# Matmuls of zeros ahead of groups for which the planned order leaves TensorE idle

## The chip, the cores and the metric

The kernel runs on one core of a Trainium2 chip. A core has five engines that run their own instruction streams side by side: TensorE (PE, matmuls; its weight loads are listed apart as PEld), VectorE (DVE), ScalarE (ACT), GpSimd (POOL) and SyncE (SP, which issues DMAs here). They meet at semaphores. The metric is the device time of one execution in microseconds; lower is better.

## The reference

The program takes eight images of 256 channels by 32 x 32 pixels and passes each through four layers, every one of the form `x = x + layer(group_norm(x))`:

```python
x = x + _L0_conv_ref(_gn(x), ...)   # attention over pixels, 8 heads of 64, q and k normalised
x = x + _L1_conv_ref(_gn(x), ...)   # 3x3 convolution, 256 to 256 channels
x = x + _L2_conv_ref(_gn(x), ...)   # 3x3 convolution, 256 to 256 channels
x = x + _L3_conv_ref(_gn(x), ...)   # a mixer block, below
```

The mixer block normalises over channels, splits the channels into four branches of 64, and runs a selective scan in each: a projection to 128 channels, a short convolution, and then for 16 states per channel the recurrence

```python
h = dA_t * h + dBu_t        # along the 1,024 pixels
y_t = einsum('bds,bs->bd', h, C_t)
```

After the branches come a gate, a chain of short depthwise convolutions with projections, attention with 8 heads of 32, a projection, layer norm, gelu, a 3 x 3 depthwise convolution, another layer norm and a last projection. All data is float32.

## The kernel before

**Tiling.** An image is two tiles of 128 partitions (channels) by 1,024 (pixels). [...]The PSUM tiles are `big` (128 x 1,024, two of them, for nearly all projections, attention scores and layer norm sums), `acc` (128 x 512, one, attention values), `cv` (128 x 512, two, convolution products and small statistics) and `y` (128 x 512, one, the sum of the scan over states).

**Stages.** For each image the parts are recorded under a letter: A (`front_attention`), O (`front_out`), C (`front_convs`), N (`scan_layers` up to the scan), S (the scan), F0 to F3 and Z0 to Z3 (front and back of each branch), B (`back_layers`, with the second attention) and E (`back_out`, `back_end`). Parts of several images are worked on side by side.

**The scan.** `scan_steps` runs over 64 units per image (4 branches, 2 halves of 512 pixels, 4 groups of states, 2 channel groups). In each, VectorE forms `hs` from `du` and `bc`, ScalarE makes the two decays `da`, VectorE scans twice, and VectorE multiplies `hs` by `bc` again. `add_up` then adds up over states on TensorE: after each second unit, four matmuls with the constant `sel` as weights, each into 32 of the 128 rows of `y`, which use 32 of the array's columns each and stand side by side. After the fourth group VectorE reads `y` in `u<-u,half_d,y`, and the next half starts on the same PSUM tile. There are four `hs` tiles.

**The order.** No engine call is issued at once. `Recorded` and `Plan.record` write every call down as an operation; `arrange` puts them in one order; `Plan.issue` then issues them in that order and ties each engine's instructions to it, so every engine runs exactly the planned sequence. That is why nearly all instructions of the profile carry one line, L252, the call in `issue`. `arrange` works on groups: `gather` joins neighbouring matmuls of a stream into groups, `appraise` gives each a duration from formulas, and a loop takes, among the engines' best candidates, the one that can start first by these durations. In it `free[e]` is the time at which engine `e` is free, `start` the time at which the chosen group can begin, `spare[room]` the times at which the buffers of a pool tag become free, and `new_tiles(n)` the buffers that group `n` would be the first to use. It also carries a picture of TensorE's clock: in `pass_windows`, with windows of `WINDOW` (3,413.33 ns), the clock is taken to halve after a window with less than 0.42 of matmul time and to recover after one with at least 0.85.

```python
def pass_windows(time):
    nonlocal window, used, warm
    while (window + 1) * WINDOW <= time:
        share = used / WINDOW
        warm = share >= 0.42 if warm else share >= 0.85
```

Where the loop starts a matmul group later than `free[0]`, TensorE is idle by the plan; before the change nothing is done about it. What the chip does at run time follows the order, not the planned times: an instruction starts when its engine has done the one before and its semaphores allow it.

## Time and profile before

| | us |
|---|---|
| three runs | 5207.44, 5217.47, 5219.44 (median 5217.47) |
| the profiled execution | 5205.82 |
| its span, first to last instruction | 5204.1 |

| engine | busy, us | share | instructions |
|---|---|---|---|
| TensorE matmuls | 4700.7 | 90% | 18,998 |
| TensorE weight loads | 1917.1 | 37% | 18,998 |
| VectorE | 4115.6 | 79% | 5,650 |
| ScalarE | 2880.8 | 55% | 3,768 |
| GpSimd | 3.3 | 0% | 18 |

The mean granted TensorE clock is 0.941 of full speed. A float32 matmul of the program shows as two records in the profile, so 18,998 records are 9,499 matmuls; a row `x4` of `y<-hs,sel` is two matmuls. The costliest groups of matmuls:

| group | records | busy, us |
|---|---|---|
| acc<-p,v (attention values) | 3,072 | 827.8 |
| cv<-taps,w (convolutions) | 3,072 | 746.0 |
| big<-q,k (attention scores) | 2,048 | 586.3 |
| y<-hs,sel (the scan's sum over states) | 2,048 | 336.9 |
| big<-ident,ln_r (a row spread over partitions) | 384 | 55.7 |

How the views are read: the page cuts the span into 40 slices of 130 us and gives each engine's busy share in tenths, with the granted clock (PEclk) below. The chain of waits starts at the last instruction and goes back, at each step to what released it or to the instruction before it on its engine; its shares say which engine the end time hangs on. The order of time lists instructions of an engine with their start and duration, and in brackets the idle time before and what ended it. A view by stretches gives busy time and the granted clock between two times.

### The profile page before, as it was taken

What the parts mean: (1) busy time and instruction counts of PE and PEld (TensorE: products, weight loads), DVE (VectorE), ACT (ScalarE), POOL (GpSimd) and SP (SyncE); (2) the same over time, 40 slices, a digit from 0 to 9 for tenths busy, and PEclk for the clock granted to TensorE, in tenths of its full rate; (3) what the DMA queues carried; (4) which work ended last, traced back from release to release, by engine and by line L of the source; (5) the groups of instructions that cost most, each with busy time, mean ns of one, the idle gap of its engine ahead of it and who ended that gap; (6) DMA issues with size and microseconds to landing.
All of it is one profiled execution on the core that took longest, in us unless ns stands there. A gap on an engine that the chain in (4) does not pass through costs nothing.

```text
span 5204.1 us, 53545 instructions
## 1 busy us (share of the span) xinstructions
PE 4700.7 (90%) x18998; PEld 1917.1 (37%) x18998; DVE 4115.6 (79%) x5650; ACT 2880.8 (55%) x3768; POOL 3.3 (0%) x18
## 2 busy tenths in 40 slices
PE   8999879989999999999999999999999899698595
PEld 3363243243432534244442444325343343232222
DVE  3335989888888968979897788888877989999903
ACT  4426445646665565646666555655656556566342
POOL 0000000000000000000000000000000000000000
PEclk9999889999999999999999999899999999798696
DMA  4133344344343433433423343324433444344100
GB/s 134 46 100 110 121 151 127 95 125 134 106 125 101 144 100 108 126 102 126 131 91 107 106 142 125 112 74 141 123 109 108 125 131 157 98 126 126 66 18 23
DMA packets 256658, 575.15 MB, mean 111 GB/s; under 512 B 51192, under 2 KB 79224, under 8 KB 256384
## 3 DMA queue, kind: packets, MB, share of 16 engines
q1 hardware_dynamic: 167680, 431.11, 26.5%
q10 hardware_dynamic: 88704, 140.55, 8.8%
q8 instruction: 152, 2.49, 0.2%
q14 instruction: 122, 1.00, 0.1%
HBM read 483.18 MB, written 63.18 MB: 105 GB/s over the span
## 4 chain that ended last, share of the span: by engine, by line
PE 64%; DVE 23%; ACT 5%; issue 4%; DMA 3%; SPq 1%; DVEq 0%; ACTq 0%
PE big L252 36%; PE cv L252 14%; DVE hs L252 13%; PE acc L252 12%; PE y L252 2%; ACT p L252 2%; DVE room L252 2%; DMA rs<-inv 1%; DVE xt L252 1%; DVE u L252 1%; DVE st L252 1%; DVE xm L252 1%; SPq L252 1%; DVE p L252 1%; ACT taps L252 1%
## 5 line engine op out<-in xcount | busy, mean ns | idle before, releaser
L252 ACT ACTIVATE p<-big 128x1024 f32<-128x1024 f32 x1024 | 1013.4, 1019 | 556.1 <-PE big L252 487.7
L252 ACT ACTIVATE da<-dt,a_neg 128x512 f32<-128x512 f32 x1024 | 727.8, 720 | 721.6 <-DVE hs L252 584.8
L252 PE MATMUL acc<-p,v 128*64 128x512 f32 x3072 | 827.8, 622 | 31.3 <-ACT p L252 28.3
L252 PE MATMUL cv<-taps,w 128*128 128x256 f32 x3072 | 746.0, 393 | 40.3 <-DVE taps L252 29.4
L252 PEld LDWEIGHTS cv<-taps,w 128*128 128x128 f32 x3072 | 580.3, 194 | 295.6 <-issue 147.2
L252 DVE TENSOR_TENSOR hs<-du,bc 128x1024 f32<-128x1024 f32 x512 | 613.4, 1210 | 73.7 <-PE y L252 61.1
L252 DVE TENSOR_TENSOR_SCAN hs<-da,carry,hs 128x512 f32<-128x512 f32 x512 | 638.1, 1271 | 9.1 <-ACT da L252 8.2
L252 DVE TENSOR_TENSOR hs<-hs,bc 128x1024 f32<-128x1024 f32 x512 | 621.7, 1214 | 18.2 <-ACT carry L252 16.6
L252 PE MATMUL big<-q,k 64*128 64x512 f32 x2048 | 586.3, 654 | 31.3 <-ACT p L252 23.0
L252 DVE TENSOR_TENSOR_SCAN hs<-da,hs 128x512 f32<-128x512 f32 x512 | 608.9, 1210 | 5.0 <-ACT da L252 3.5
L252 DVE TENSOR_TENSOR p<-p 128x1024 f32<-128x1024 f32 x256 | 311.8, 1218 | 227.6 <-ACT p L252 164.7
L252 PE MATMUL y<-hs,sel 128*32 128x512 f32 x2048 | 336.9, 643 | 121.2 <-DVE hs L252 119.3
L252 PEld LDWEIGHTS acc<-p,v 128*64 128x64 f32 x3072 | 161.3, 136 | 590.7 <-issue 415.7
L252 PEld LDWEIGHTS big<-q,k 64*128 64x128 f32 x2048 | 160.3, 189 | 427.7 <-issue 207.7
L252 PE MATMUL big<-qk,qk 32*128 32x512 f32 x2048 | 298.1, 645 | 3.1 <-ACT qk L252 2.2
L252 PE MATMUL cv<-p,v 128*64 128x512 f32 x1024 | 276.9, 612 | 0.0
L252 PE MATMUL big<-xn,w 128*128 128x512 f32 x512 | 232.8, 600 | 2.8 <-ACT v L252 2.5
L252 PE MATMUL big<-o,w 128*128 128x512 f32 x384 | 182.5, 621 | 12.5 <-DVE o L252 12.2
L252 PEld LDWEIGHTS y<-hs,sel 128*32 128x32 f32 x2048 | 50.1, 111 | 337.8 <-DVE hs L252 187.6
L252 DVE SCALAR_TENSOR_TENSOR room<-room,vec,room 128x992 f32<-128x992 f32 (+1 forms) x128 | 156.7, 1224 | 10.0 <-ACT room L252 9.2
L252 PEld LDWEIGHTS big<-qk,qk 32*128 32x128 f32 x2048 | 82.3, 184 | 187.2 <-issue 140.1
L252 PEld LDWEIGHTS big<-xn,w 128*128 128x128 f32 x512 | 94.0, 190 | 130.0 <-issue 115.2
(234 smaller groups left out, 5038.5 us busy)
## 6 DMA issues: line engine op xcount, KB each, us to landing
bc<-bc SPq DMA_DIRECT2D x256, 512.0 KB
w<-wc ACTq DMA_DIRECT2D x384, 256.0 KB
dt<-dt_m SPq DMA_DIRECT2D x128, 512.0 KB
du<-du_m SPq DMA_DIRECT2D x128, 512.0 KB
rs<-inv SPq DMA_DIRECT2D x64, 256.0 KB
raw<-xm SPq DMA_DIRECT2D x64, 256.0 KB
dt_m<-dt SPq DMA_DIRECT2D x128, 128.0 KB
du_m<-a SPq DMA_DIRECT2D x128, 128.0 KB
```

The lines of the kernel that those rows point to most:

```text
L252: made = op["call"](*args, **kwargs).ins
```

## The change

`arrange` now notes, when it takes a matmul group (`e == 0`) that starts over 1,000 ns after TensorE is free by the plan, whose first output has at least 128 elements a partition and lies in a pool tile whose buffer is free by then, a count: `0.75 * idle - 500` ns, divided by 220 ns. `issue` issues that many calls of `fill` ahead of the group's first matmul, each tied into TensorE's order like any other. `fill` calls the same matmul with a 128 x 128 tile of zeros as weights (as many rows and columns as the real matmul uses) and 128 columns of the identity as moving data, into the first 128 columns of the place that the group's first matmul will write. Where that matmul starts a sum, so does the fill, and is overwritten; where it continues one, the fill adds zeros. The order of all other operations, and the count of everything else, is as before.

```diff
+            for call in [self.fill] * idle + [op["call"]]:
+                made = (call(op) if call == self.fill else call(*args, **kwargs)).ins
...
+    def fill(self, op):
+
+        out, lhs = op["outs"][0], op["ins"][0]
+        rows = slice(region(lhs)[1], region(lhs)[2])
+        zeros, moving = self.still
+        moving = moving[rows]
+        if len(out.shape) == 3:
+            wide = out.shape[2]
+            out = out[:, 0 : P // wide]
+            moving = moving.rearrange("p (h w) -> p h w", w=wide)
+        else:
+            out = out[:, 0:P]
+        start = op["args"][1]["start"]
+        return op["call"](
+            out, zeros[rows, 0 : out.shape[0]], moving, start=start, stop=start
+        )
...
+        if e == 0 and start - free[0] > 1000.0 and elements(ops[g.ops[0]]["outs"][0]) >= P:
+            new, out = new_tiles(n), ops[g.ops[0]]["outs"][0].tensor.name
+            since = max([sorted(spare[r])[len(t) - 1] for r, t in new.items()] + [0.0])
+            if out in rooms and since <= free[0]:
+                idle[n] = int((0.75 * (start - free[0]) - 500.0) / 220.0)
...
+    zeros = wp.tile([P, P], F32, name="zeros")
+    nc.gpsimd.memset(zeros, 0.0)
+    plan.still = zeros, ident
```

In the issued program this makes 1,064 matmuls of zeros in 87 places, among 9,499 others.

## The prediction

> **What bounds the kernel now.** I read the page's slices and its chain of work that ended last, then clock and busy time by stretch, then TensorE's order of time around each place where the change adds work.

> ```profile
> PE   8999879989999999999999999999999899698595
> ...
> DVE  3335989888888968979897788888877989999903
> ...
> PEclk9999889999999999999999999899999999798696
> ...
> PE 64%; DVE 23%; ACT 5%; issue 4%; DMA 3%; SPq 1%; DVEq 0%; ACTq 0%
> ```

> TensorE holds most of the chain, but not all: in slices 5 and 35 to 38 VectorE is at 9 tenths while TensorE falls to 5 or 6. TensorE is idle for 488 us in all (345 us of it in gaps over 2 us), and its clock is granted at half for 621 us, 394 of them with TensorE busy, 243 of those on the chain. So the ceiling of everything a warm clock could give is 243/2 = 121 us. What drops the clock is shown by four stretches of 3.41 us, the step in which the clock's changes stand in this trace, and a long one for later (from:to; length; busy time of TensorE, its loads, VectorE, ScalarE, GpSimd; granted clock; DMA):

> ```profile
> 1059.20:1062.61 3.41, 1.05 (x4) 0.17 (x4) 3.41 (x4) 3.37 (x4) 0.00 (x0) 1.00 0.00 0
> 1062.61:1066.03 3.42, 3.03 (x4) 1.48 (x5) 3.31 (x7) 0.91 (x2) 0.00 (x0) 0.51 0.17 37
> 410.58:413.99 3.41, 3.41 (x29) 2.73 (x25) 1.23 (x1) 0.81 (x1) 0.00 (x0) 1.00 0.06 7
> ...
> 2687.28:2690.70 3.42, 3.42 (x33) 3.40 (x31) 3.42 (x7) 1.56 (x2) 0.00 (x0) 1.00 0.03 2
> ...
> 4824.10:4895.78 71.68, 22.35 (x44) 3.87 (x40) 71.68 (x81) 23.06 (x32) 0.00 (x0) 0.52 0.20 66
> ```

> The third stretch is busy throughout, with matmuls of one column (cv<-mean_w,ln_sq) in most of it; the clock is at half from 414.0 on all the same. The first has w_mxpw alone, 32 of 128 columns of the array, and drops too. The fourth is half such one-column matmuls and half transposes by the identity (128 columns of the array), and holds its clock. Weighing each matmul's streaming time by the rows and columns it uses, I find no drop above a share of 0.37 and nearly no hold below it. A half clock ended only after a stretch of some 0.75 or more. These two numbers are my reading of this trace, an estimate.

> **The added work, its price.** The changed program's order has 1,064 extra matmuls ahead of 87 groups, and no other engine's order changes but for one 128x128 clearing on GpSimd at the start (its like, ident, took 0.20 us; GpSimd is done at 3.94 us, TensorE's first matmul starts at 7.85). By shape: 421 into big, 152 into cv (128 columns of the array), 414 into y and 26 into big (32 columns), 51 with 64. Each streams 128 columns, as the transposes do (eight matmuls, two records each):

> ```profile
> 4818.53 3.78 PE L252 MATMUL big<-ident,ln_r 128*128 128x128 f32 x16 [1.77 <-DVE ln_r L252]
> ...
> 4912.35 2.02 PE L252 MATMUL big<-ident,ln_r 128*128 128x128 f32 x16 [1.20 <-DVE ln_r L252]
> ```

> Less about 0.3 us for the last one's end, that is 0.43 us each at half clock and 0.22 at full. 1,064 x 0.223 = 237 us. I set each block against the idle time that the trace shows at that place: 143 us fit into it, 94 do not. Of the 94, y blocks make 64: they cost 92 us and find 28. So the order that the planner believes in and the trace agree for wide blocks and disagree for y, where the real TensorE is usually still behind. A block also takes over the wait for its PSUM tile's last reader; that wait stood there before, on the group itself, so it costs nothing new until the block is longer than the group's other wait. All later matmuls queue behind it, and in-order ScalarE (p, then da) and VectorE behind those.

> **What it gains.** Blocks of 128 columns lift these stretches over 0.37, and the half clock that followed goes; on the chain it held TensorE for 4.6 us (from 707.6), 4.8 (1349.3), 3.4 (629.1), 2.8 (1670.1), 3.1 (2264.1), 2.7 (3059.4), 3.0 (4933.3), 3.8 (5093.7) and 3.1 (4780, after the block itself). Sum 31.3 us; at full clock half of it, **15.6 us**. The rest of the 243 stays: one-column and narrow matmuls cause some (414.0, 878.3, 3185.7, 3274.4, 5172.2), others have gaps without a block.

> [...]The first row above had a gap of only 2.38 us and 1.05 us of 32-column matmuls, and dropped. [...]

> **What it loses, place by place** (lateness that reaches the chain, 0.223 or 0.43 us a fill by the clock of that stretch):

> - 4809 to 4900, where VectorE is busy 71.68 of 71.68 us and the clock is 0.52. These are TensorE's rows before:

> ```profile
> 4822.24 2.33 PE L252 MATMUL y<-hs,sel 128*32 128x512 f32 x8
> 4829.85 1.92 PE L252 MATMUL y<-hs,sel 128*32 128x512 f32 x4 [5.27 <-DVE hs L252]
> 4836.95 1.92 PE L252 MATMUL y<-hs,sel 128*32 128x512 f32 x4 [5.19 <-DVE hs L252]
> 4841.74 1.92 PE L252 MATMUL y<-hs,sel 128*32 128x512 f32 x4 [2.86 <-DVE hs L252]
> 4846.52 1.92 PE L252 MATMUL y<-hs,sel 128*32 128x512 f32 x4 [2.86 <-DVE hs L252]
> ...
> 4848.94 0.75 DVE L252 SCALAR_TENSOR_TENSOR u<-u,half_d,y 128x512 f32<-128x512 f32 x1
> ```

>   Ahead of the y at 4809.19 stand 24 fills: cold, 10.2 us, to 4819.3; two y rows, three fills and the transposes follow and end near 4828.3 instead of 4822.3. VectorE's room<-room,big stood at 4822.90 with no idle time: 5.4 us late. Then (times without that shift) 39 fills from 4824.57: 13 warm, 26 cold, to 4838.6; the y rows of 4829.85 and 4836.95 to 4842.4; 25 fills to 4853.1; the next two y rows to 4857.0. VectorE's u at 4848.94 reads that y: 8.1 us more. Last, 49 fills (20.9 us) and 42 wide ones (some 12, warming on the way) make the mean matmuls end at 4909.3; VectorE's room at 4896.8, by now 8.1 late, waits 4.4 more. Sum **17.8 us**. Were y to warm the clock, this place would cost about nothing.
> - 1072.7: 43 fills and 10 more before cv<-taps,w at 1090.65; 15 warm, the rest cold, end 1096.2. 5.5 late, but cv then runs warm where it was cold for 6 us: +2.5.
> - 482.7: 38 fills, 8.5 us, against 2.21 and 3.65 us idle: +2.6 and 3.1 saved if the clock holds (share 0.41, a close call), +7.9 if not: +2.4 taken.
> - 617 to 670, seven blocks: between 0 and 5.9: 2 taken, near the low end since 9.24 us of idle time follow at 704.
> - 3762: +1. 4411 to 4464 (y 4, 10 and 9 fills, big 12): lateness of 4 to 6 before a chain that leaves by y and u at 4461.6: +4.
> - Twenty fills between two TensorE pieces of the chain (654, 1733, 2298, 2575, 4957): 4.5. Excess over short waits for taps (304, 367, 2325, 2543): 3.0.

> Everything else is late against slack and caught by the next gap, the 113 fills at 5129 (25 to 28 us in 22.28, then 9.45 more idle) among it. If that cover were gone, the whole 94 us would count, and cold blocks more. Losses: 17.8 + 2.5 + 2.4 + 2 + 1 + 4 + 4.5 + 3.0 = **37.2 us**. Net +21.6 on the profiled execution's 5205.8 us (span 5204.1): 5227. That execution was the shortest seen, 0.2% under the median of the three runs, 5217.5; the same sum on the median gives **5239**.

> **Rivals.**
> - Nothing measurable. For it: most lateness falls where TensorE waits for VectorE anyway, so if only the 17.8 us of the end pass on, gain and loss are 15.6 and 17.8: 5220. Against it: ScalarE serves exp for attention and da for the scan in one order, so a late TensorE reaches VectorE's scan soon.
> - Faster, by narrow fills that count as activity: the end place costs nothing, 1072.7 is absorbed, and the gain is 15.6 + 4.7 + 2.5 (mean matmuls at 4891 warm) = 22.8; with 3 of lateness left, 5197. It decides if the clock over 4824 to 4896 rises to near 1; below a net of 16 us it turns into the case above. Against it: the w_mxpw row.
> - Much slower, zeros not counting at all: the page shows no zero operand. The gains go, and wide blocks run cold over their idle time (32 at 704: 13.7 us in 9.24; 113 at 5129: 48 in 31.7; five more), some 27 us beyond the 37: 5217.5 + 64 = 5281.
> - The change doing half of what it says (44 of 87 blocks longer than the idle time there) is part of my forecast, not a rival.

> **The numbers.** A measurement of this kernel tells no change from about 0.3%, 16 us: 5202 to 5233. Forecast 0.43 and the much slower case 0.10 make slower 0.53; nothing measurable 0.25; faster 0.22. The range, 5197 to 5285, leaves out the far part of the faster case and of full lateness. The likeliest case alone: 5233 to 5270.

> **What will show it.** TensorE's busy time up by about 237 us, with y fills at 0.43 us and a clock still near 0.5 in the stretch before the last image's u; the mean clock, 0.941, little changed; VectorE waiting for y or big there (it waited 61.1 us for y in all before); the spells after 704, 1346 and 5090 gone. Wrong would be a clock near 1 under y fills alone (then the faster case), or half clock under the 113 wide ones (then zeros don't count).

## The result: slightly faster, and the profile after

Twelve runs of the changed kernel have a median of 5199.18 us (5191.64 to 5210.09), twelve of the kernel before 5215.65 us (5205.63 to 5225.01). The ratio is 0.9971, with a 95% interval of 0.996 to 0.9981: faster by 0.29%, where 0.4% slower was forecast. The profiled execution's span went from 5204.1 to 5193.1 us, 11.0 less.

Lines of the page of the changed kernel: busy times, then slices of TensorE, VectorE and the granted clock, the chain's shares by engine, and two of the costliest groups:

```profile
PE 4884.4 (94%) x21126; PEld 2149.3 (41%) x21126; DVE 4114.9 (79%) x5650; ACT 2880.1 (55%) x3768; POOL 3.5 (0%) x19
...
PE   8999899999999999999999999999999999799798
...
DVE  3335989888888968979797788888887989999813
...
PEclk9999999999999999999999999999999999899898
...
PE 64%; DVE 24%; ACT 5%; issue 3%; DMA 3%; SPq 1%; DVEq 0%; ACTq 0%
...
L253 DVE TENSOR_TENSOR hs<-du,bc 128x1024 f32<-128x1024 f32 x512 | 613.0, 1209 | 72.1 <-PE y L253 59.0
...
L253 PE MATMUL y<-hs,sel 128*32 128x512 f32 x2048 | 322.6, 626 | 48.7 <-DVE hs L253 46.7
```

The 2,128 further records are the 1,064 fills. TensorE's slices are full nearly everywhere, the clock's digits too, and the slices of VectorE stay nearly as they were. The mean granted clock rose from 0.941 to 0.966, and the time at half clock fell from 621 to 358 us. VectorE waited 59.0 us for y ahead of hs, against 61.1 before: the fills into y did not make it wait longer. TensorE's busy time rose by 184 us, 53 less than the 237 us that the fills were priced at; the real work that ran at half clock fell from 394 to 259 us.

**Where the time went.** VectorE runs the same instructions in the same order in both traces, so the start of each against its start before is a curve of gain and loss. It stands at -2.3 us at 560, goes back to -0.4 at 739, to -4.0 at 1403, -7.5 at 2300, -5.6 at 4198, -8.8 at 4804, -7.9 at 4906, -7.4 at 5168 and -11.0 at the end. The stretch that was to lose 17.8 us, 4804 to 4906, lost 0.9. TensorE's time at half clock on the chain fell from 242.8 to 211.2 us; half of the difference is 15.8 us, and 28.3 us of fills now stand on the chain themselves.

**What the narrow fills did there.** Order of time of the changed kernel on TensorE, fills in L278; everything stands some 9 us earlier than before (the two y rows shown stood at 4850.97 and 4858.93):

```profile
4800.33 6.67 PE L278 MATMUL y<-ident,zeros 128*32 128x128 f32 x47
...
4814.65 8.13 PE L278 MATMUL y<-ident,zeros 128*32 128x128 f32 x73
...
4842.11 1.92 PE L253 MATMUL y<-hs,sel 128*32 128x512 f32 x4 [3.40 <-DVE hs L253]
4850.07 1.07 PE L253 MATMUL y<-hs,sel 128*32 128x512 f32 x2 [6.04 <-DVE hs L253]
...
4850.94 11.98 PE L278 MATMUL y<-ident,zeros 128*32 128x128 f32 x93
...
4868.56 10.99 PE L278 MATMUL big<-ident,zeros 128*128 128x128 f32 x84
```

And stretches of 3.41 us in which TensorE does nothing but such 32-column fills; only in the third do two y records stand beside the first of them (from:to; length; busy time and records of TensorE and its loads, of the fills alone; granted clock; DMA):

```profile
4803.14:4806.55 3.41, 3.41 (x33) 3.41 (x32) 1.00 0.00 0
4816.79:4820.20 3.41, 3.41 (x33) 3.41 (x32) 1.00 0.12 41
4850.93:4854.34 3.41, 3.41 (x18) 2.83 (x16) 0.50 0.78 255
4854.35:4857.76 3.41, 3.41 (x33) 3.41 (x32) 1.00 0.15 58
4414.02:4417.43 3.41, 3.41 (x18) 2.83 (x17) 0.50 0.03 5
```

Where the clock was full it stayed full (1.00 at 4803, 4816 and 4854). Where it was at half, one stretch of 32-column fills brought it back: the third is at 0.50 and the fourth, next in time, at 1.00; the last is at 0.50, and the clock is full from 4417.4 on. The whole place, 4815.40 to 4887.90, which is the prediction's stretch of 4824 to 4896, with all engines as there, has a clock of 0.84, where it was 0.52:

```profile
4815.40:4887.90 72.50, 51.34 (x349) 39.77 (x347) 72.50 (x80) 23.66 (x32) 0.00 (x0) 0.84 0.20 66
```

Of all 2,128 fill records only some 180 ran at half clock.

**The shares, read again.** So in these rows 32 columns of the array did what the prediction gave to 128 alone. I took the streaming time of each matmul again (eight 512-column records, such as big<-local,w at 5102.20, take 3.60 us, from which I estimate 0.43 us for 512 columns and 0.107 for 128), doubled it at half clock (16 records of the transposes took 3.78 us there and 2.02 at full), weighed it by rows alone, and counted matmuls that stand side by side on other columns once (eight records of y<-hs,sel took 1.07 us at 1070.92), those on other rows together. I summed it by windows of 3.41 us: the granted clock changes 139 times in the trace before and 113 times in that of the changed kernel, always between 1.0 and 0.5 of full speed, and any two changes of a trace lie a whole multiple of 3.41 us apart. In both traces, the clock was never seen to drop above a share of some 0.39 or to hold below 0.36; it rose from some 0.7 upward, and stayed at half up to 0.78. With columns weighed as well, the changed kernel's windows hold at 0.2 and rise from 0.25, while others drop at 0.37 and stay at half at 0.7, so that no line parts them. These shares are estimates; the two in `pass_windows` are the planner's, and no run tests them. The row that decided the prediction (1059.20, w_mxpw) fits: its two matmuls run side by side (four records in 1.05 us, where four of big<-u,mdtw at 1718.82 of the changed kernel took 1.98), so 1.05 us of busy time hold about 0.86 us of streaming, 0.25 of the stretch, with any weight for columns. This was only a reading, made after the result; experiments test it.

### The profile page after: what moved, and what is told of

It is laid out like the page before. It is cut to its first block, busy times and chain, and to the rows that moved or that the text cites. A ratio compares the mean times of both kernels' runs of the same rounds, so it can differ in the third digit from the quotient of the medians.

```text
span 5193.1 us, 57793 instructions
## 1 busy us (share of the span) xinstructions
PE 4884.4 (94%) x21126; PEld 2149.3 (41%) x21126; DVE 4114.9 (79%) x5650; ACT 2880.1 (55%) x3768; POOL 3.5 (0%) x19
## 4 chain that ended last, share of the span: by engine, by line
PE 64%; DVE 24%; ACT 5%; issue 3%; DMA 3%; SPq 1%; DVEq 0%; ACTq 0%
PE big L253 35%; PE cv L253 14%; DVE hs L253 14%; PE acc L253 12%; PE y L253 3%; ACT p L253 2%; DVE room L253 2%; DMA rs<-inv 1%; DVE xt L253 1%; DVE u L253 1%; DVE st L253 1%; DVE p L253 1%; DVE dt L253 1%; ACT taps L253 1%; DVE fd L253 1%
## 5 line engine op out<-in xcount | busy, mean ns | idle before, releaser
L253 PE MATMUL acc<-p,v 128*64 128x512 f32 x3072 | 825.1, 620 | 23.9 <-ACT p L253 20.9
L253 PE MATMUL y<-hs,sel 128*32 128x512 f32 x2048 | 322.6, 626 | 48.7 <-DVE hs L253 46.7
```

Of the source, the lines that this page charges most:

```text
L253: made = (call(op) if call == self.fill else call(*args, **kwargs)).ins
```

## The experiments

Ratios are against the kernel before, run on the same chip in between. The first four change the fills of the changed kernel alone, so that the computation is the same.

**One column instead of 128.** The fills stay in number and place, and stream one column.

```diff
         moving = moving[rows]
+        moving = moving[:, 0:1]
...
-            out = out[:, 0:P]
+            out = out[:, 0:1]
```

> The same 1,064 extra matmuls in the same places, but each streams one column instead of 128 (a chain of one-column matmuls has the same step, 0.22 us at full clock, 0.43 at half). Theory T (the gain is the clock, and a fill holds it by the time it streams): the clock falls back to about 0.94, the gain goes, and the y blocks now run cold, so the lateness that was predicted comes true: 5230 to 5260 us, ratio 1.003 to 1.008. Rival O (the gain is not the clock but something else that comes with a filled queue): about 5199 us, ratio 0.997.

Measured: 5252.25 us, ratio 1.0075 [1.0063, 1.0087], clock 0.938. The order of time of this kernel (fills in L277):

```profile
4825.46 2.67 PE L277 MATMUL y<-ident,zeros 128*32 128x1 f32 x47
...
4894.30 18.08 PE L277 MATMUL big<-ident,zeros 128*128 128x1 f32 x84
```

The second row is the same 84 records as at 4868.56 above. They leave no gap for 18 us, and the clock stays at half (from 4844.09 to 4915.77): 0.215 us each. With one column to stream, these fills kept TensorE busy for 18.08 us and left its clock at half. The whole place as a stretch (columns as above, with VectorE, ScalarE and GpSimd after the loads) has the clock of the kernel before again, where the changed kernel had 0.84:

```profile
4840.40:4916.70 76.30, 45.34 (x353) 31.77 (x348) 72.78 (x80) 24.49 (x33) 0.00 (x0) 0.53 0.20 62
```

**32 rows instead of all.** The fills stream their 128 columns, through 32 rows of the array.

```diff
-        rows = slice(region(lhs)[1], region(lhs)[2])
+        rows = slice(region(lhs)[1], region(lhs)[1] + 32)
```

> All fills, but with 32 rows of zeros and identity instead of 128 (same columns streamed, same time each). Theory R (in both traces a share weighed by rows, not by columns, parts the stretches that drop from those that hold, at 0.37): 32 rows weigh a quarter, so the clock falls back to 0.94 to 0.95 and the y blocks run cold: 5225 to 5260 us, ratio 1.002 to 1.008. Rival (any streaming time counts in full): clock 0.966, 5199 us, ratio 0.997.

Measured: 5269.79 us, ratio 1.0099 [1.0086, 1.0113], clock 0.938, a little beyond what the rows' theory gave and far from its rival. In order of time:

```profile
4895.44 21.11 PE L278 MATMUL y<-ident,zeros 32*32 32x128 f32 x98
...
4918.34 18.29 PE L278 MATMUL big<-ident,zeros 32*128 32x128 f32 x84
```

Both are blocks that the changed kernel did in about 12 (93 of the first's 98 records in 11.98) and 10.99 us. The columns are as many, only the rows are fewer, and the clock over this place (4852.20 to 4940.50) is 0.54. With these fills cold, VectorE's lateness between 4803 and 4906 grew from 28.1 to 45.5 us: by 17.4, which is the 17.8 us of the prediction. The total of its working held for cold fills (at half clock), but by some luck: the steps at 4823, 4849 and 4897 are 3.9, 2.7 and 10.8 us, where it had 5.4, 8.1 and 4.4, and the wide fills, which it let warm up in some 12 us, took 18.29. In the changed kernel the fills were not cold.

**Only wide, only narrow.** The condition in `arrange` is narrowed to groups that use over 32 columns of the array, or at most 32.

```diff
-            if out in rooms and since <= free[0]:
+            if out in rooms and since <= free[0] and g.array[1] > 32:
```

> Fills only where the group's matmuls use more than 32 columns of the array: 624 of the 1,064. Theory T (columns don't matter): the clock gives back about half of its rise (0.950 to 0.958), time between both kernels, 5199 to 5210 us, ratio 0.997 to 0.999. Rival C (a fill of 32 columns counts a quarter, as predicted): leaving the narrow ones out costs no clock (0.966 stays) and saves their lateness: 5180 to 5190 us.

> Fills only where the group's matmuls use 32 columns: 440 of the 1,064. Theory T: the narrow ones hold and wake the clock by themselves: clock 0.950 to 0.958, 5202 to 5213 us, ratio 0.9975 to 0.9995. Rival C: clock about 0.94, only lateness: 5230 to 5250 us, ratio 1.003 to 1.007.

Measured: wide alone 5202.05 us, ratio 0.9978 [0.9969, 0.9988], clock 0.956; narrow alone (`<= 32`) 5203.41 us, 0.9979 [0.9969, 0.999], clock 0.951. The 440 narrow fills, which I had down for most of the loss, gain as much as the 624 wide ones. Together they gain less than the sum (0.29% against 0.43%), which is within what the intervals leave open.

**Longer and shorter blocks.** The count of the changed kernel is `0.75 * idle - 500` ns over 220. The first form makes 1,330 fills of it, the second 550.

```diff
-                idle[n] = int((0.75 * (start - free[0]) - 500.0) / 220.0)
+                idle[n] = int((start - free[0] - 900.0) / 220.0)
...
+                idle[n] = int((0.4 * (start - free[0]) - 250.0) / 220.0)
```

> The changed kernel with fills for the whole planned idle time less 0.9 us (1,330 fills ahead of 82 groups instead of 1,064 ahead of 87). Theory T: the windows held at full clock are held already at 0.75 of the idle time, so 266 further fills bring little clock (0.965 to 0.972) and wherever the planned idle time is longer than the real one they delay the group: 5195 to 5215 us, ratio 0.996 to 1.000. Rival M (more fill, more clock): 5180 to 5192 us, clock above 0.975.

> The changed kernel with fills for 0.4 of the planned idle time (550 fills ahead of 82 groups). Theory T: a window needs about 0.37 of its time streamed to hold the clock and 0.75 to rise, so fills at 0.4 at one end of the gap leave whole windows empty and hold few: 5205 to 5220 us, ratio 0.998 to 1.0005, clock 0.945 to 0.957. Rival G (any work in the gap resets the gate): as with all fills, 5190 to 5202 us, clock 0.962 to 0.968.

Measured: 1,330 fills 5195.38 us, ratio 0.9966 [0.9952, 0.9981], clock 0.969; 550 fills 5198.42 us, 0.9978 [0.9969, 0.9987], clock 0.955. The longer blocks came out as expected: no more than the change itself, with 104 us of fills on their chain. With the shorter ones my theory had the clock right and the time wrong (5205 to 5220 expected), and the rival, any work in the gap, the time right and the clock wrong: half of the fills gain nearly as much. The one-column fills, at 5252.25 us and a clock of 0.938, speak against that rival. In their trace only 2.1 us of fills lie on the chain, against 28.3; but TensorE's time at half clock on the chain is as long as before (244.6 us), so the lateness saved does not explain the whole. That part stays open.

**The other cause of half clock.** By the same shares the layer norms' column sums should drop the clock without any gap: they stream one column. In the kernel before, 32 such records stand from 411.26 and the clock is at half from 414.0. The next kernels widen them, without fills and with, and read the first column of each sum. The 128-column form streams the whole of mean_w and writes its columns 48 apart (`i * 48 : i * 48 + P`), so that eight sums fit in 512 columns and each next one overwrites only what is not read; the planner is told the old duration, so that the order stays.

```diff
-                    pv[:, i : i + 1],
+                    pv[:, i * 64 : i * 64 + 64],
...
-                    mean_w[:, 0:1],
+                    mean_w[:, 0:64],
...
-        vector.tensor_scalar_add(r, pv[:, 0:NKT], 1e-5)
+        vector.tensor_scalar_add(r, pv[:, 0 : 64 * NKT : 64], 1e-5)
```

> The kernel before, without any fill; the column sums of the layer norms (mean_w with ln_sq or room) stream 64 columns of mean_w instead of one, and the first column of each 64 is read. Theory T (the clock follows the time in which TensorE streams, weighed by rows): a one-column matmul is bound by its weight load and hardly streams, so a window of them counts as idle and drops the clock, in some 22 spells with about 128 us of cold TensorE on the chain; with 64 columns the step stays at 111 ns and about 0.48 of it streams, more than the 0.37 that holds the clock. It expects 5145 to 5185 us, a ratio of 0.987 to 0.994, a clock of 0.96 or more, and no drop in the windows of these sums. Rival W (the busy share of the records decides, or the spells come from the layer norms' waits for VectorE): nothing measurable, ratio 0.998 to 1.002, clock 0.941. Rival D (a 64-column fp32 matmul takes twice the step): slower, ratio above 1.003.

> The changed kernel with the same 64-column sums. Theory T: both gains add, since they act in different windows, and the fills beside the sums find a clock that is already full: 10 to 20 us below the 64-column kernel without fills, 5130 to 5170 us, ratio 0.983 to 0.991, clock 0.98 or more. Rival S (both act on the same spells): the same time as the better of the two alone, within 3 us.

> The kernel before, without fills, with the layer norms' column sums streaming 128 columns of mean_w (written 48 columns apart, so that each group's sums stay in its first column). Theory T: a 128-column matmul has the step of a one-column one (the fills' records are as long as the sums'), so the time of the sums does not change, and they now stream for nearly all of it: they not only hold the clock, as 64 columns do, but can raise it. It expects the time of the 64-column kernel or up to 15 us less, 5170 to 5187 us, ratio 0.992 to 0.9955, clock 0.947 to 0.960. Rival D (128 columns cost more than the weight load): slower than with 64 columns, above 5192 us.

> The changed kernel with the 128-column sums. Theory T: at most as long as with 64 columns and all fills, 5155 to 5173 us, ratio 0.989 to 0.9925, clock 0.972 to 0.980. Rival D: above 5178 us.

> The 128-column sums with fills for 0.4 of the planned idle time. If fills at 0.4 do as much as at 0.75, as the kernels with one-column sums came out, the time is that of the kernel with all fills and 128-column sums within 5 us, 5155 to 5175 us. If the further fills are worth their clock, it lies 5 to 12 us above it.

| kernel | median, us | ratio [95%] | clock | at half clock, us | of it TensorE on the chain, us | span against before, us |
|---|---|---|---|---|---|---|
| before | 5215.65 | 1 | 0.941 | 621 | 242.8 | 0 |
| changed | 5199.18 | 0.9971 [0.996, 0.9981] | 0.966 | 358 | 211.2 | -11.0 |
| 64 columns, no fills | 5186.45 | 0.9952 [0.9939, 0.9966] | 0.946 | 563 | 192.9 | -24.3 |
| 64 columns, fills | 5171.79 | 0.9922 [0.9909, 0.9935] | 0.972 | 287 | 169.9 | -33.5 |
| 128 columns, no fills | 5167.29 | 0.9917 [0.9904, 0.9931] | 0.950 | 516 | 153.5 | -39.6 |
| 128 columns, 560 fills | 5154.27 | 0.9892 [0.9877, 0.9907] | 0.969 | 325 | 98.7 | -53.6 |
| 128 columns, 1,083 fills | 5146.09 | 0.9876 [0.9861, 0.9891] | 0.980 | 209 | 96.5 | -56.5 |

TensorE around the sums of 411 us, of the kernel before and then of the one with 128 columns and no fills:

```profile
411.26 4.47 PE L252 MATMUL cv<-mean_w,ln_sq 128*128 128x1 f32 x32
415.67 4.63 PE L252 MATMUL big<-q,k 64*128 64x512 f32 x10
```

```profile
412.09 3.84 PE L252 MATMUL cv<-mean_w,ln_sq 128*128 128x128 f32 x32
415.86 1.99 PE L252 MATMUL big<-q,k 64*128 64x512 f32 x8
```

The stretch behind, in the same two kernels (columns as before):

```profile
414.00:417.41 3.41, 3.41 (x13) 2.49 (x15) 1.89 (x13) 0.00 (x0) 0.00 (x0) 0.51 0.03 4
```

```profile
414.04:417.45 3.41, 3.41 (x25) 2.39 (x24) 1.77 (x12) 0.41 (x1) 0.00 (x0) 1.00 0.06 6
```

The clock falls at 414.0, during the first row, and stays full through the second and behind it. The same 32 records stream 128 times as much and take no longer (the end of the first row ran at half clock), and q,k behind them takes 0.25 us a record instead of 0.46. For the kernel without fills, the half of what left the chain at half clock, (242.8 - 153.5) / 2 = 44.7 us, is close to the 39.6 us of the span; with 64 columns, 24.9 against 24.3. With 128 columns and fills the same half is 73 and, with the 560 fills, 72 us, well over the 56.5 and 53.6 of the spans; why is open.

Not all of it was foreseen. With 64 columns the time, 5186, just missed the range of the theory (5145 to 5185), and the clock, 0.946, missed by far (0.96): I had put some 128 us of the chain down to the sums, and 50 went. Many of those windows have other gaps too, and 64 columns stream for 0.48 of the time by my estimate, between the shares above at which the clock dropped (up to some 0.39) and rose (from some 0.7). With 128 columns the mean clock was 0.950 instead of 0.946, and they gained another 0.35%, some 18 us, more than the 15 that I had allowed. The kernel with 64 columns and fills too came out just past its range and under its clock, that with 128 columns and all fills 9 us below its range. The two causes are separate ones: all fills take 21 us from the kernel with 128 columns, and 0.4 of the idle time takes 13 of these. The further 8 us lie in the 5 to 12 that I had named for the case that the further fills are worth their clock; with four runs of each, the intervals of the two ratios still overlap. The page of the kernel with all fills and 128 columns, busy time, clock and chain:

```profile
PE 4829.2 (94%) x21164; PEld 2114.7 (41%) x21164; DVE 4112.6 (80%) x5650; ACT 2879.9 (56%) x3768; POOL 3.5 (0%) x19
...
PEclk9999999999999999999999999999999999999999
...
PE 64%; DVE 24%; ACT 5%; issue 4%; DMA 3%; SPq 1%; DVEq 0%; ACTq 0%
```

The clock's digits are 9 to the end, with 55 us less of TensorE than in the changed kernel and 19 more fills. It beats both the kernel before and the changed one: 1.2% faster than before.

## Why the prediction was wrong

Held against its own steps:

- **Bounds**: right. TensorE still has 64% of the chain, and what moved the time was its clock: with fills that did not hold it (one column, 32 rows: clock 0.938 in both) the gain is gone (ratios 1.0075 and 1.0099).
- **Price of a fill**: right. The block at 5121.40 has 113 fills in 25.40 us, 0.225 us each, where I put 25 to 28; TensorE still had 7.68 us to wait for VectorE's room a little later (9.45 forecast), so the cover that I named for it held.

```profile
5121.40 25.40 PE L278 MATMUL big<-ident,zeros 128*128 128x128 f32 x226
```

- **Zeros**: they counted. The rival in which they don't falls: the clock is 1.00 in the stretches at 4803.14, 4816.79 and 4854.35, which hold nothing but fills of zeros.
- **Gain**: 15.6 us forecast, 15.8 by the chain's time at half clock. That they meet is partly chance: of the nine spells listed, 629, 1670, 2264, 4780 and 4933 went (the curve gains 1.4 and 3.5 us at 1670 and 2264), 1349 and 5093 kept 3.4 and 2.9 us on the chain, 3059 stayed and 707 did not go at all, and the spell at 482 went, which I had taken as lost.
- **The weight of columns**: this is the step that failed. The prediction weighs matmuls by the columns of the array too, and so has fills of 32 columns stay cold where the clock is at half (26 of 39 at 4824.57). I had read two things, rows and columns, into one row of the trace in which only one stretch spoke for columns, and that one had a second reading: matmuls side by side, counted twice. In the changed kernel the narrow fills held a full clock (4803.14, 4816.79) and ended a half one (4850.93 to 4857.76), so the largest term, **17.8 us at 4809 to 4900, was 0.9**, all of it behind 4900. The terms built on the same step fell with it: 482.7 (2.4 forecast) was -0.2, as 75 of its 76 records ran in 8.38 us, at full clock; 1072.7 (2.5) was 1.0 over the whole of 1040 to 1101, and cv<-taps,w came no later; 4411 to 4464 (4) was 0.8. The trace before held other rows on this question, and they spoke against columns (the prediction's columns):

```profile
622.30:625.71 3.41, 1.83 (x8) 0.16 (x6) 3.41 (x7) 2.39 (x5) 0.00 (x0) 1.00 0.00 0
625.72:629.13 3.41, 1.52 (x7) 0.92 (x6) 3.41 (x9) 3.41 (x11) 0.00 (x0) 0.99 0.52 163
...
3059.40:3062.81 3.41, 2.71 (x4) 0.75 (x4) 3.41 (x7) 0.94 (x3) 0.00 (x0) 0.50 0.08 14
3062.82:3066.23 3.41, 0.51 (x2) 0.00 (x0) 3.29 (x5) 2.86 (x4) 0.00 (x0) 1.00 0.00 0
```

  The first stretch holds y<-hs,sel alone, 32 columns each and two side by side. By rows TensorE streams for nearly half of it, with columns weighed for under 0.3, and the clock stays full. The third holds big<-u,w_moutw alone, 64 of 128 columns: a share of some 0.8 by rows, of at most 0.40 with columns, and the clock rises. So the prediction's two numbers, 0.37 and 0.75, do not come out of its own trace by the weight that it used.

- **The smaller losses**: 617 to 740 was sized well. It lost 2.5 us by the curve, where I had taken 2 for 617 to 670. The 7.5 us for fills between TensorE pieces and ahead of taps can't be read singly; all losses together are about 15.8 - 11.0 = 4.8 us, where I had 37.2.

The rival that won is the one I gave 0.22: narrow fills that count as activity, 5197 us, though its sum, 22.8 us gained and 3 lost, is more than the 16.5 of the medians and the 11.0 of the spans. No run shows its term of 4.7 us. By the trace before it is half of the time for which TensorE held the chain at half clock at two places, 6.06 us between 1035 and 1110 and 3.41 us from 1721.3; in the trace of the changed kernel that was 6.83 us between 1035 and 1110 and none between 1700 and 1740. The test of this rival was named, the clock over 4824 to 4896, and read 0.84. Measured from its median the change gave 0.29%, at the edge of what I had called no change; twelve runs of each resolve it.

Idle time of TensorE did not tell what the clock did either. The one-column fills of 4894.30 to 4912.38 leave no gap, and the clock stays at half; in the kernel before, the one-column sums at 411.26 leave none (TensorE is busy for 3.41 of 3.41 us from 410.58), and the clock is at 0.51 in the stretch behind. What went with the clock in these runs is how much of a stretch is streamed (one column or 128: clock 0.938 or 0.966), and through how many rows (32 or all: 0.938 or 0.966).

## What to carry to other kernels

A busy TensorE wasn't a warm one here (busy throughout from 410.58, and at half clock from 414.0): look in the trace for runs of matmuls with one or few columns, or few rows, right ahead of each fall of the clock, and try to let them stream more columns where the trace shows that their step does not grow (here 3.84 us for 32 records of 128 columns, 3.79 for 64), before filling any gap. The width of a fill in the array cost nothing here: 440 fills of 32 columns gained 0.21%, 624 wider ones 0.22%, so that even a narrow place in PSUM could take one; with 32 rows or with one column the fills lost 0.99% and 0.75%. And where a prediction rests on one row of a trace, look for a second row that differs in that one property before choosing it over everything else.
